# Other TensorE work between a product and its copy-out, and a fixed ScalarE order, in a four-stage kernel

## The chip, the cores and the metric

The kernel runs on one core of a Trainium2 chip. The metric is the time of one execution on the device, in microseconds. Five engines work beside each other, each in the order of its own queue: TensorE (PE, with its weight loads shown as PEld), VectorE (DVE), ScalarE (ACT), GpSimd (POOL) and SyncE (SP), which here issues the transfers. TensorE writes to PSUM; ScalarE and VectorE read it from there.

## The reference, cut to what matters

Four images of 512 channels and 64 x 64 points go through four layers. All is computed in float32. The change is in the first stage (layer 0) and at the start and end of the last one (layers 2 and 3):

```python
# layer 0: attention over the 4096 points of an image, d = 64
t = einsum('oc,bchw->bohw', w_qkv, x)            # key, query, value: 64 channels each
scores = einsum('bdk,bdq->bkq', key_, query)
attn = softmax(scores, axis=1)
out = einsum('bdk,bkq->bdq', value, attn)
x = scale * einsum('oc,bchw->bohw', w_out, out) + x
# layer 1: a bottleneck block whose weights are mixed from 8 experts by a router on mean(x)
# layer 2: linear attention with softplus features, divided by its norm
# layer 3: x + gamma * gate * sigmoid(discounted cumulative sums along rows and columns)
```

## The kernel before, where the change touches it

An image is held as four pairs of 512-point blocks, `xs[0]` to `xs[3]`. Keys and queries of two pairs at a time are computed as a 2 x 2 block product with seven multiplications in place of eight. `self.w[k]` are sums of weights, `term(.., k, ..)` sums of x. Four of the seven (1, 6, 7, 4) are added up in one PSUM bank `y`, and between them `y` is copied out as it stands: `seed` after 1, `e2` after 6, `e3` after 7. The next product goes on adding in the same bank, so it waits until the copy has read it. The three others (5, 2, 3) are added up in `zy`.

```python
class Projections:
    ...
        def steps(self, b):
            first = "v1 cp01 v2 5 1 seed t6 t4 n5 6 e2 2 c11 n6 tr01 7 e3 c22 v3a n7 4 c21 3 c12 n4"
            if b == 0:
                first = "zero v0 1 seed t5 v1 cp01 t6 5 2 c11 t7 t4 n5 6 e2 n6 tr01 v2 7 e3 c22 v3a n7 4 c21 3 c12 n4"
            return first.split(), "5 1 seed 6 e2 2 c11 v3b cp23 7 e3 c22 tr23 4 c21 3 c12".split()
    ...
    def products(self, xs, pair, steps, key, qry, vt):
        ...

            def to_key(src, pr, own=True):
                for h in range(2):
                    n0 = (2 * pr + h) * NB
                    for to in range(2):
                        if own or to != h:
                            nc.scalar.copy(key[to * D:(to + 1) * D, n0:n0 + NB], src(h, n0))
        for step in steps:
            ...
                if step == "zero":

                    nc.tensor.matmul(zy[:, 0, :], ident, wqkv_sb.rearrange("p k o -> p (k o)")[:, 0:NB],
                                     start=True, stop=True)
                elif step.isdigit():
                    k = int(step)
                    to = y if k in (1, 6, 7, 4) else zy[:, 0 if k == 2 else 1, :]
                    for c in range(2):
                        for h in range(2):
                            nc.tensor.matmul(to[h * D:(h + 1) * D, :], self.w[k][:, c, :],
                                             self.term(xs, pair, k, c)[:, h * NB:(h + 1) * NB],
                                             start=c == 0 and k in (1, 5), stop=c == 1,
                                             skip_group_check=k not in (1, 5))
                elif step == "seed":
                    nc.scalar.copy(zy[:, 0, :], y)
                elif step in ("e2", "e3"):
                    e[step] = block(f"{step}_{self.b}_{pair[0]}")
                    nc.scalar.copy(e[step], y)
                elif step == "c11":
                    to_key(lambda h, n0: zy[h * D:(h + 1) * D, 0, :], pair[0])
                elif step == "c12":
                    for h in range(2):
                        r, n0 = slice(h * D, (h + 1) * D), (2 * pair[1] + h) * NB
                        nc.vector.tensor_tensor(key[r, n0:n0 + NB], zy[r, 1, :], e["e2"][r, :], ALU.add)
                    to_key(lambda h, n0: key[h * D:(h + 1) * D, n0:n0 + NB], pair[1], own=False)
                elif step == "c21":
                    nc.vector.tensor_copy(qry[:, pair[0] * NB:(pair[0] + 1) * NB], y)
            ...
```

The steps are words: a digit is one product (four matmuls of 64 x 512), `v` a value product of a pair (eight matmuls), `cp` and `tr` the copy and the transposes of values, `t` and `n` the sums of x on VectorE for this pair and for the next one, `c11` to `c22` the copies of finished blocks to `key` and `qry`. VectorE and ScalarE run this part in program order, TensorE the whole kernel.

Then come the scores, in groups of six, and with each group the value matmuls of the group before:

```python
        def pool(pr, kc):
            xm = xs[pr][:, kc, :]
            nc.scalar.activation(xm, xm, AF.Copy, accum_out=pool_acc[:, kc, pr:pr + 1])
        ...
        for g, group in enumerate(groups):
            for i in group:
                scores(i)
            if 1 < g < 2 + 2 * KC:
                pool(NPAIR - 2 + (g - 2) // KC, (g - 2) % KC)
            if g == 0:
                if b == 0:
                    router_of_values()
                continue
            for _ in range(2):
                if late and late[0][0] < g:
                    late.pop(0)[1]()
            for n, i in enumerate(groups[g - 1]):
                if g == len(groups) - 1 and n == 4:
                    inverse_sums(NPAIR - 1)
                pr = values(i)
                if pr is not None:
                    late.append((g, lambda pr=pr: sums(pr)))
                    if pr < NPAIR - 2:
                        late += [(g + 1, lambda pr=pr, m=m: out_step(pr, m)) for m in range(KC)]
```

`scores(i)` makes two matmuls into one of three PSUM pair buffers, an exp on ScalarE into a ring of twelve, and an addition on VectorE. ScalarE's order here is chosen by the scheduler. `router_of_values` transposes `w_out`, has VectorE copy it, and multiplies it by the router's weights.

The last layer runs through tiles. Its products are seven again, for the sums (`s`) and for the gates (`g`) of a tile, and their orders are lists of words, in which `q` takes a leftover of layer 2 and `v` the first value product of the next image:

```python
        steps = (("s1", "s seed", "l rows 1"), ("g1", "g seed", "y", "l rows 0", "l turn 1"),
                 ("s5", "l turn 0", "a", "q"), ("g5", "l columns 1"),
                 ("s6", "s copy_out 2", "l columns 0", "y"), ("g6", "g copy_out 2", "l sigmoid 1", "a"),
                 ...
        last_steps = (("g5", "l rows 1", "l rows 0"), ("g1", "g seed"), ("g6", "g copy_out 2", "l turn 1"), ("g2",),
                      ("g7", "g copy_out 3", "l columns 1", "g fourth", "l turn 0", "l columns 0", "l sigmoid 1",
                       "l sigmoid 0", "v"), ("g4",), ("g3", "x", "g third", "g first", "g second"))
```

Here `y` is a product of layer 2 into a pair buffer and `a` its addition to x on VectorE (L827). In the second round of tiles the last `q` is the division by the norm: a matmul `nrm` (L760) into a pair buffer and a multiply on VectorE (L763).

## Time and profile before

| | |
|---|---|
| time, median of 3 runs | 2700.67 us (2700.61 to 2700.9) |
| span of the profiled execution | 2698.4 us |
| mean TensorE clock granted | 0.997 |
| matmul `s` of the scores, L354, busy | 466.9 us |
| first score matmul, batch 0 and batch 1 | 56.63 us and 730.50 us |
| transfers, mean over the span | 43 GB/s |

The profile gives each engine's busy time and its share of the span. Its timeline lists instructions in order of time: start, duration, engine, line of the kernel, operation, written tile <- read tiles, shapes, and a count where alike ones are merged. In brackets stands how long the engine was idle before, and what released it. A float32 matmul appears as two records, so a count of 8 is four matmuls of the program. Starts tell more than durations, since matmuls overlap. The granted clock is the share of full speed that TensorE was allowed.

### The profile page before, as it was taken

How to read it: one execution, taken by the hardware profiler on the slowest of the kernel's cores; microseconds unless marked ns; L12 is line 12 of the kernel's file. 1: busy time of each engine (PE TensorE's matmuls, PEld its weight loads, DVE VectorE, ACT ScalarE, POOL GpSimd, SP SyncE). 2: the span in 40 equal slices, each digit the busy share in tenths (PEclk: the TensorE clock that was granted, in tenths of full speed). 3: DMA queues.
4: the chain of work that ended last, by engine and by line, in shares of the span. 5: the costliest groups of instructions: out<-in, count | busy, mean ns of one | idle time of the engine just before them, and what ended most of it. 6: DMA issues, size and time to landing. Idle time of an engine off the chain costs nothing.

```text
span 2698.4 us, 25783 instructions
## 1 busy us (share of the span) xinstructions
PE 2650.6 (98%) x10048; PEld 1114.0 (41%) x10048; DVE 2013.2 (75%) x2270; ACT 1318.2 (49%) x1511; POOL 11.8 (0%) x26
## 2 busy tenths in 40 slices
PE   7999999999999999999999999999999999999998
PEld 2333365344333346434433334543443333554443
DVE  5678766788678876678877878668886777856787
ACT  4555353545655435345565453535556555353545
POOL 1000000000000000000000000000000000000000
PEclk9999999999999999999999999999999999999999
DMA  5000210022200021002220002001121000210011
GB/s 190 1 1 1 102 32 1 16 90 82 94 1 1 1 102 32 1 24 101 78 78 1 0 1 102 32 1 59 66 84 72 0 1 1 102 32 0 32 47 48
DMA packets 34595, 115.17 MB, mean 43 GB/s; under 512 B 2976, under 2 KB 12192, under 8 KB 32928
## 3 DMA queue, kind: packets, MB, share of 16 engines
q1 hardware_dynamic: 34464, 113.43, 11.2%
q8 instruction: 81, 1.33, 0.2%
q14 instruction: 50, 0.41, 0.0%
HBM read 79.86 MB, written 33.55 MB: 42 GB/s over the span
## 4 chain that ended last, share of the span: by engine, by line
PE 89%; DVE 5%; ACT 4%; DMA 1%; issue 1%; SPq 0%; DVEq 0%; ACTq 0%
PE av L369 17%; PE s L354 17%; PE sx L904 14%; PE zy L904 10%; PE z L648 4%; PE c L623 4%; PE c L551 4%; PE c L600 3%; PE wv L822 2%; PE y L413 2%; PE g L724 2%; PE xtr L709 2%; PE kq L296 2%; PE c2e L600 2%; PE vv L252 1%; DVE s L937 1%
## 5 line engine op out<-in xcount | busy, mean ns | idle before, releaser
L354 PE MATMUL s<-qv,key 64*128 64x512 f32 x2048 | 466.9, 602 | 3.4 <-ACT ring L357 3.4
L362 DVE TENSOR_TENSOR acc<-acc,ring 128x1024 f32<-128x1024 f32 x312 | 381.7, 1223 | 95.0 <-ACT ring L357 65.2
L357 ACT ACTIVATE ring<-s 128x1024 f32<-128x1024 f32 x336 | 317.1, 1039 | 210.6 <-PE s L354 210.6
L369 PE MATMUL av<-ring,qv 128*64 128x512 f32 x1344 | 304.5, 595 | 0.0
L354 PEld LDWEIGHTS s<-qv,key 64*128 64x128 f32 x2048 | 188.6, 187 | 279.5 <-issue 171.0
L362 DVE TENSOR_TENSOR acc<-acc,x 128x1024 f32<-128x1024 f32 x168 | 205.6, 1224 | 102.5 <-ACT x L357 89.5
L357 ACT ACTIVATE x<-s 128x1024 f32<-128x1024 f32 x176 | 171.7, 1040 | 203.2 <-PE s L354 203.2
L904 PE MATMUL sx<-t,x 128*128 128x512 f32 x512 | 237.7, 598 | 3.3 <-ACT zy L909 2.5
L369 PEld LDWEIGHTS av<-ring,qv 128*64 128x64 f32 x1344 | 93.3, 137 | 198.6 <-issue 198.6
L369 PE MATMUL av<-x,qv 128*64 128x512 f32 x704 | 167.2, 598 | 0.0
L909 ACT COPY zy<-sx 128x512 f32<-128x512 f32 x64 | 36.5, 570 | 265.8 <-PE sx L904 256.3
L904 PEld LDWEIGHTS sx<-t,x 128*128 128x128 f32 x512 | 95.1, 190 | 133.3 <-issue 117.4
L954 DVE TENSOR_TENSOR_SCAN t<-x,t 128x512 f32<-128x512 f32 x128 | 148.8, 1209 | 1.6
L943 ACT COPY t<-s 128x1024 f32<-128x1024 f32 x64 | 127.5, 1992 | 42.0 <-DVE s L937 41.4
L937 DVE TENSOR_TENSOR_SCAN s<-wc,s 128x512 f32<-128x512 f32 x128 | 146.0, 1202 | 0.0
L913 ACT ACTIVATE e<-sx,prm_sb 128x512 f32<-128x512 f32 x128 | 86.9, 685 | 108.6 <-PE sx L904 108.6
L960 ACT ACTIVATE s<-t 128x1024 f32<-128x1024 f32 x64 | 125.6, 1988 | 12.0 <-DVE t L954 12.0
L904 PE MATMUL zy<-t,wq 128*128 128x512 f32 x256 | 119.3, 604 | 0.0
L904 PE MATMUL sx<-t,wq 128*128 128x512 f32 x256 | 117.0, 597 | 2.1 <-ACT e L913 2.1
L904 PE MATMUL sx<-x,wq 128*128 128x512 f32 x256 | 117.1, 596 | 0.0
L904 PE MATMUL zy<-x,x 128*128 128x512 f32 x256 | 116.2, 594 | 0.0
L648 PE MATMUL z<-x,wqk_sb 128*64 128x512 f32 x512 | 115.9, 597 | 0.0
(229 smaller groups left out, 3443.6 us busy)
## 6 DMA issues: line engine op xcount, KB each, us to landing
out_dram<-s SPq DMA_DIRECT2D x64, 512.0 KB, 2.6
x<-in_x_dram SPq DMA_DIRECT2D x14, 2048.0 KB, 8.6
ex<-in_packed_dram SPq DMA_DIRECT2D x4, 2048.0 KB, 7.5
ex<-in_experts_dram SPq DMA_DIRECT2D x4, 2048.0 KB, 7.8
wq<-in_wproj_t_dram SPq DMA_DIRECT2D x32, 256.0 KB, 5.0
ex<-in_packed_dram SPq DMA_DIRECT2D x4, 1536.0 KB, 6.1
ex<-in_experts_dram SPq DMA_DIRECT2D x4, 1536.0 KB, 6.6
x<-in_packed_dram SPq DMA_DIRECT2D x4, 1536.0 KB, 8.3
```

The source lines that it names most:

```text
L354: nc.tensor.matmul(s[:, h, :], key[r, kt * P:(kt + 1) * P], qry[r, pr * NB:(pr + 1) * NB], start=True, stop=True)
L357: nc.scalar.activation(p, s, AF.Exp)
L362: nc.vector.tensor_tensor(accs[pr], accs[pr], p, ALU.add)
L369: nc.tensor.matmul(avs[pr][h * D:(h + 1) * D, :], vt[:, kt, :], ring[i % RING][:, h, :], start=kt == 0, stop=kt == NT - 1)
L551: nc.tensor.matmul(y[:, h, :], wc[:, kc, :], xs[pr][:, kc, h * NB:(h + 1) * NB], start=kc == 0, stop=kc == KC - 1)
L600: nc.tensor.matmul(y[:, lo - a:hi - a], u, v[:, lo:hi], start=dy == 1, stop=dy == 2)
L648: nc.tensor.matmul(z[h * D:(h + 1) * D, i, :], wqk_sb[:, kc, w * D:(w + 1) * D], xs[pair[i]][:, kc, h * NB:(h + 1) * NB], start=kc == 0, s ...
L904: nc.tensor.matmul(y, w[:, c, self.kind, self.j * P:(self.j + 1) * P], v[:, c, :], start=c == 0 and k in (1, 5), stop=c == 1, skip_group_c ...
L937: nc.vector.tensor_tensor_scan(self.half(i, h), along[:, self.j + 2 * i, :], self.half(i, h), 0.0, ALU.mult, ALU.add)
L943: nc.scalar.copy(self.t[i].rearrange("p (w r) -> p w r", w=W), self.s[i].rearrange("p (r w) -> p w r", w=W))
L954: nc.vector.tensor_tensor_scan(th, down[:, i, :], th, 0.0, ALU.mult, ALU.add)
L960: nc.scalar.activation(self.s[i].rearrange("p (r w) -> p w r", w=W), tw, AF.Sigmoid)
```

## The change

It gives each product that follows a copy of its own partial sum some other TensorE work to do first. In the first stage's step lists, `v2` comes between 1 and 6 and the transposes between 7 and 4. In the second pair of pairs half a value product comes behind 1. The key copies through SBUF (`c12`) are put off, to the place of `k` and behind the first group of exps. VectorE takes `c22` ahead of sums for later products. In the last layer half of the value product moves behind `g1`, and `q` moves one product later.

ScalarE is held to program order in the score loop too, so the pooling passes and key copies stand where the program has them. For the first batch, whose data come while it starts, the order is its own: parameters are loaded ahead of x, the zeroing matmul reads only the identity, and the router's product follows the first values.

```diff
-    xs = [load_pair(0, pr) for pr in range(NPAIR)]
-
-    a11, a12, a21, a22 = (...)
-    nc.vector.tensor_tensor(a21, a21, a22, ALU.add)
     prm_sb = const.tile([P, NPRM], F32, tag="prm", name="prm_sb")
     nc.sync.dma_start(prm_sb, prm)
+    xs = [load_pair(0, pr) for pr in range(NPAIR)]
+
+    a11, a12, a21, a22 = (...)
     ...                                     # after the constants:
+    nc.vector.tensor_tensor(a21, a21, a22, ALU.add)
     ...                                     # router_of_values: the product is returned, with a buffer of its own
+        def products():
+            wr = pair_psum("wr_p")[:, 0, 0:E]
     ...                                     # Projections.steps
-            first = "v1 cp01 v2 5 1 seed t6 t4 n5 6 e2 2 c11 n6 tr01 7 e3 c22 v3a n7 4 c21 3 c12 n4"
+            first = "v1 cp01 5 1 seed v2 t6 t4 n5 6 n6 e2 2 7 e3 c11 c22 tr01 n7 4 c21 3 c12 n4"
             if b == 0:
-                first = "zero v0 1 seed t5 v1 cp01 t6 5 2 c11 t7 t4 n5 6 e2 n6 tr01 v2 7 e3 c22 v3a n7 4 c21 3 c12 n4"
-            return first.split(), "5 1 seed 6 e2 2 c11 v3b cp23 7 e3 c22 tr23 4 c21 3 c12".split()
+                first = "zero v0 1 seed t5 v1 cp01 t6 5 2 t7 t4 6 e2 v2 7 e3 c11 c22 tr01 n5 n6 n7 4 c21 3 c12 n4"
+            return first.split(), "5 1 seed k v3a 6 e2 2 v3b cp23 7 e3 c11 c22 tr23 4 c21 3 c12".split()
     ...                                     # products: zero
-                    nc.tensor.matmul(zy[:, 0, :], ident, wqkv_sb.rearrange("p k o -> p (k o)")[:, 0:NB],
-                                     start=True, stop=True)
+                    nc.tensor.matmul(zy[:, 0, :].rearrange("p (j c) -> p j c", c=P), ident,
+                                     ident[:, None, :].to_broadcast([P, TPB, P]), start=True, stop=True)
     ...                                     # products: c12, and the new step k
-                    to_key(lambda h, n0: key[h * D:(h + 1) * D, n0:n0 + NB], pair[1], own=False)
+                    self.left.append(lambda: to_key(lambda h, n0: key[h * D:(h + 1) * D, n0:n0 + NB], pair[1],
+                                                    own=False))
+                elif step == "k":
+                    self.key_copies()
     ...                                     # the score loop
+        with tc.manual_schedule(engines={mybir.EngineType.Activation}):
             for g, group in enumerate(groups):
                 ...
                 if g == 0:
+                    pro.key_copies()
                     if b == 0:
-                        router_of_values()
+                        router = router_of_values()
                     continue
                 ...
+                if b == 0 and g == 1:
+                    router()
     ...                                     # the last layer
-                 ("s5", "l turn 0", "a", "q"), ("g5", "l columns 1"),
+                 ("s5", "l turn 0", "a"), ("g5", "l columns 1", "q"),
     ...
-        last_steps = (("g5", "l rows 1", "l rows 0"), ("g1", "g seed"), ...
+        last_steps = (("g5", "l rows 1", "l rows 0"), ("g1", "g seed", "v 0"), ...
-                       "l sigmoid 0", "v"), ...
+                       "l sigmoid 0", "v 2"), ...
-                            pro.value(nxt, 0)
+                            pro.value(nxt, 0, int(args[0]), 2)
```

More of the change, by code (lines that the diff above doesn't have):

```diff
@@ L99, in unshifted @@
     nc.sync.dma_start(wqkv_sb, wqkv_t.rearrange("(kc p) o -> p kc o", p=P))
-    xs = [load_pair(0, pr) for pr in range(NPAIR)]
-    a11, a12, a21, a22 = (wqkv_sb[:, k:k + 2, w * D:(w + 1) * D] for w in range(2) for k in (0, 2))
-    nc.vector.tensor_tensor(a21, a21, a22, ALU.add)
     prm_sb = const.tile([P, NPRM], F32, tag="prm", name="prm_sb")
@@ L107, in col @@
         return prm_sb[:, i:i + n]
+    xs = [load_pair(0, pr) for pr in range(NPAIR)]
+    a11, a12, a21, a22 = (wqkv_sb[:, k:k + 2, w * D:(w + 1) * D] for w in range(2) for k in (0, 2))
     wout_sb = const.tile([P, C], F32, tag="wout", name="wout_sb")
@@ L173, in router_of_values @@
         nc.vector.tensor_copy(wot_sb, wo_t[:, 0, :])
-        for kc in range(KC):
-            nc.tensor.matmul(wo_t[:, 1, 0:E], wot_sb[:, kc * P:(kc + 1) * P], router_sb[:, kc, :],
-                             start=kc == 0, stop=kc == KC - 1)
-        nc.vector.tensor_scalar(wr_sb, wo_t[:, 1, 0:E], col(SCALE), 1.0 / HW, ALU.mult, ALU.mult)
+        def products():
+            wr = pair_psum("wr_p")[:, 0, 0:E]
+            for kc in range(KC):
+                nc.tensor.matmul(wr, wot_sb[:, kc * P:(kc + 1) * P], router_sb[:, kc, :],
+                                 start=kc == 0, stop=kc == KC - 1)
+            nc.vector.tensor_scalar(wr_sb, wr, col(SCALE), 1.0 / HW, ALU.mult, ALU.mult)
+        return products
     def load_experts(b, j, n, pool, tag, pack=True):
@@ L214, in __init__ @@
             self.sums = bigp.tile([P, 4, 2, NB], F32, tag="big", name=f"ring_{b}")
-            self.fours, self.vv, self.vsb = [], {}, {}
+            self.fours, self.vv, self.vsb, self.left = [], {}, {}, []
         def sum_weights(self):
@@ L225, in steps, with key_copies @@
         def steps(self, b):
[L226 removed]
+            first = "v1 cp01 5 1 seed v2 t6 t4 n5 6 n6 e2 2 7 e3 c11 c22 tr01 n7 4 c21 3 c12 n4"
             if b == 0:
[L228 to L229 removed]
+                first = "zero v0 1 seed t5 v1 cp01 t6 5 2 t7 t4 6 e2 v2 7 e3 c11 c22 tr01 n5 n6 n7 4 c21 3 c12 n4"
+            return first.split(), "5 1 seed k v3a 6 e2 2 v3b cp23 7 e3 c11 c22 tr23 4 c21 3 c12".split()
+        def key_copies(self):
+            while self.left:
+                self.left.pop(0)()
         def term(self, xs, pair, k, c):
@@ L434, in layer0 @@
         late = []
-        for g, group in enumerate(groups):
-            for i in group:
-                scores(i)
-            if 1 < g < 2 + 2 * KC:
-                pool(NPAIR - 2 + (g - 2) // KC, (g - 2) % KC)
-            if g == 0:
-                if b == 0:
-                    router_of_values()
-                continue
-            for _ in range(2):
-                if late and late[0][0] < g:
-                    late.pop(0)[1]()
-            for n, i in enumerate(groups[g - 1]):
-                if g == len(groups) - 1 and n == 4:
-                    inverse_sums(NPAIR - 1)
-                pr = values(i)
-                if pr is not None:
-                    late.append((g, lambda pr=pr: sums(pr)))
-                    if pr < NPAIR - 2:
-                        late += [(g + 1, lambda pr=pr, m=m: out_step(pr, m)) for m in range(KC)]
+        with tc.manual_schedule(engines={mybir.EngineType.Activation}):
+            for g, group in enumerate(groups):
+                for i in group:
+                    scores(i)
+                if 1 < g < 2 + 2 * KC:
+                    pool(NPAIR - 2 + (g - 2) // KC, (g - 2) % KC)
+                if g == 0:
+                    pro.key_copies()
+                    if b == 0:
+                        router = router_of_values()
+                    continue
+                for _ in range(2):
+                    if late and late[0][0] < g:
+                        late.pop(0)[1]()
+                for n, i in enumerate(groups[g - 1]):
+                    if g == len(groups) - 1 and n == 4:
+                        inverse_sums(NPAIR - 1)
+                    pr = values(i)
+                    if pr is not None:
+                        late.append((g, lambda pr=pr: sums(pr)))
+                        if pr < NPAIR - 2:
+                            late += [(g + 1, lambda pr=pr, m=m: out_step(pr, m)) for m in range(KC)]
+                if b == 0 and g == 1:
+                    router()
         assert not [t for t in late if t[0] < len(groups) - 1], late
@@ L999, in layer3 @@
                        ("s3", "s second"))
-        last_steps = (("g5", "l rows 1", "l rows 0"), ("g1", "g seed"), ("g6", "g copy_out 2", "l turn 1"), ("g2",),
+        last_steps = (("g5", "l rows 1", "l rows 0"), ("g1", "g seed", "v 0"), ("g6", "g copy_out 2", "l turn 1"), ("g2",),
                       ("g7", "g copy_out 3", "l columns 1", "g fourth", "l turn 0", "l columns 0", "l sigmoid 1",
-                       "l sigmoid 0", "v"), ("g4",), ("g3", "x", "g third", "g first", "g second"))
+                       "l sigmoid 0", "v 2"), ("g4",), ("g3", "x", "g third", "g first", "g second"))
         pro = None
```

## The prediction, made before the changed kernel ran

> **What bounds the kernel now.** I read the busy totals first, then the chain that ended last, then TensorE's timeline for the whole span, keeping only the rows with an idle time, and last ScalarE's timeline around the largest of those gaps. The totals and the head of the chain:
>
> ```profile
> PE 2650.6 (98%) x10048; PEld 1114.0 (41%) x10048; DVE 2013.2 (75%) x2270; ACT 1318.2 (49%) x1511; POOL 11.8 (0%) x26
> PE 89%; DVE 5%; ACT 4%; DMA 1%; issue 1%; SPq 0%; DVEq 0%; ACTq 0%
> ```
>
> TensorE is busy for all but 2698.4 - 2650.6 = 47.8 us. The change adds no arithmetic and takes almost none away, so those 47.8 us, and matmuls run at a reduced clock, are all it can win: 54 us, the 2%, is out of reach. TensorE's timeline shows where some of the idle time is. Batch 0, then batch 1 (batches 2 and 3 repeat it to 0.02 us):
>
> ```profile
> 30.59 1.94 PE L296 MATMUL kq<-ring,wqkv_sb 128*64 128x512 f32 x8 [0.59 <-ACT e L304]
> 34.35 1.94 PE L296 MATMUL kqz<-x,kqw 128*64 128x512 f32 x8 [1.82 <-DVE qv L315]
> 42.57 3.51 PE L296 MATMUL kq<-ring,kqw 128*64 128x512 f32 x8 [2.85 <-ACT kqz L301]
> 53.05 1.94 PE L296 MATMUL kq<-ring,wqkv_sb 128*64 128x512 f32 x8 [0.80 <-ACT e L304]
> 56.63 2.85 PE L354 MATMUL s<-qv,key 64*128 64x512 f32 x12
> 60.33 2.94 PE L354 MATMUL s<-qv,key 64*128 64x512 f32 x12 [0.85 <-ACT ring L357]
> 67.21 1.87 PE L175 MATMUL wo_t<-router_sb,wot_sb 128*128 128x8 f32 x8 [3.35 <-DVE wot_sb L173]
> ...
> 497.53 1.13 PE L760 MATMUL nrm<-inv,spread 32*128 32x512 f32 x4 [1.18 <-DVE x L827]
> ...
> 678.08 1.98 PE L904 MATMUL sx<-t,x 128*128 128x512 f32 x4 [0.66 <-ACT zy L909]
> 702.00 1.94 PE L296 MATMUL kq<-ring,kqw 128*64 128x512 f32 x8 [0.67 <-ACT kqz L301]
> 718.01 1.94 PE L296 MATMUL kq<-ring,kqw 128*64 128x512 f32 x8 [0.87 <-ACT kqz L301]
> 726.92 1.94 PE L296 MATMUL kq<-ring,wqkv_sb 128*64 128x512 f32 x8 [0.79 <-ACT e L304]
> 734.20 8.40 PE L354 MATMUL s<-qv,key 64*128 64x512 f32 x36 [0.85 <-ACT ring L357]
> ```
>
> Start, duration, line, in brackets the idle time and its releaser. Each gap at L296 is a product that waits until its own partial sum has been copied out (`seed` L301, `e2`/`e3` L304). The 2.85 us at 42.57 are more than one copy: ScalarE, in order, first did this:
>
> ```profile
> 39.56 1.30 ACT L282 COPY key<-key 64x512 f32<-64x512 f32 x2
> 40.88 1.06 ACT L431 ACTIVATE x<-x 128x1024 f32<-128x1024 f32 x1
> 41.85 0.19 ACT L431 ACTIVATION_READ_ACCUMULATOR x<-x 128x1 f32 x1
> 41.94 0.58 ACT L301 COPY kqz<-kq 128x512 f32<-128x512 f32 x1
> ```
>
> The product ended at about 39.7; key copies and a pooling pass (L431) stood ahead of the seed.
>
> **What the Trainium skill says.** "TensorE: Matmul & The Clock Gate", What's actually happening: the array runs at half clock after an idle window of some 3.4 us and at full clock after as long a busy one. The trace agrees in kind: after 2.85 us idle eight matmuls took 3.51 us against 1.89, and after the 3.35 us at 67.21 the next 24 scores took 7.35 (chain) against 5.35. "ScalarE: Activation LUTs", What ACT_TABLE_LOAD costs: about 1283 ns a load; here 1.28 (23.33 and 28.66, around the square root of L153, ahead of an `e3`). "SBUF — State Buffer", two separate sides: a GpSimd instruction and a VectorE one with two SBUF inputs lock each other out. Agrees: the two subtractions at 34.21, beside GpSimd's L120 (31.61 to 37.81), took 4.08 together; the same kind took 2.35.
>
> **The change part by part.** Units from the timeline: a product of eight 1.72 us, a value product 3.43 (half: 1.72), a value transpose 1.05, a 512-wide copy 0.58, two SBUF subtractions 2.35, a score 0.89, an exp 0.92 to 0.93 in a run (3.73 for four).
>
> *Batches 1 to 3, from the last tile of the stage before.* Half a value product now stands behind `g1`; it covers its seed (0.57), so the 0.66 goes. But `g6`, its `copy_out`, `turn` and the scans behind start 1.0 later (half a product 1.72 minus the 0.66). Hence the last sigmoid ends at 694.7 instead of 693.8, the table load at 696.0, the two value copies at about 697.1. The second value product, now between `1` and `6`, takes over the PSUM buffer that these copies free (its instruction in the built program waits for ScalarE). TensorE reaches it at 696.85: a new wait of about 0.25. It covers the seed (0.67 gone). I put `6` at 700.6 (702.00 before: 1.4 won). Then `2` 702.4, `7` 704.15, transposes 705.9, `4` 706.95: `e3` is done at 706.7. `3` at 708.7 needs `c22` on VectorE, behind four subtractions that wait for the load of pair 3. That load is issued when the last scan ends (691.57, now 692.5) and lands 10.6 later plus issue, 703.4; 703.4 + 4.6 + 0.65 = 708.7, just in time. The pair (2,3): 7 x 1.72 + 3.43 + 1.05 with some 0.09 per wait or switch puts the first score at 727.5 (730.50 before: 3.0). Every copy there has at least 1.05 us of other work behind it, and the key copies that held the first exp (731.97 to 733.2) now stand behind six exps. They then delay exp 7 by 1.2, of which TensorE sees about 1.0 in the first twelve scores (before 0.85 plus 0.3 stretch). Won per batch: 3.1, all three 9.3.
>
> *Batch 0.* From 16.64, the end of the second value product's issue, I add 0.4 for the parameter load now ahead of x (25 KB, issue slot 0.5) and for the clock, since the zeroing product now needs only the identity (ready at 1.4) and will be over before x lands. So 17.05. Then 5, 2, 6: 22.2; v2 25.7; 7 27.4; transposes 28.4; 4 30.2; 3 31.9; 5, 1, v3a 37.0; 6 38.8; 2, v3b 42.2. The subtractions for pair 3 are now behind `c22` and the value copies, so they start at 30.05, not 26.97, and run into GpSimd's L120: I take them to be held some 3.4 us (the lock from 32.4 to 35.8). 6 just manages, but `c12` ends at about 42.3, the key copies at 43.5, and `e2` stands behind them, 44.1: `7` waits 1 to 1.8. Then 7, transposes, 4, 3 = 6.2, and the first score at about 50.5 against 56.63: 6.1 won. Gone are 0.59 + 1.82 + 2.85 + 0.80 and the 1.79 lost to the clock (7.85); up to 1.8 come back.
>
> From first score to first values product 19.8 us passed before (56.63 to 76.44). Now: twelve scores and four transposes are 11.3; the third of the ring's PSUM buffers waits for VectorE's copy of `wo_t` (at about 8.3 + 0.7 after the first score, behind four additions of 1.33), 1.2; exp pace the rest, in all 12.6. The router products come after the values, some 0.6. 19.8 - 13.2 = 6.6 won, 2.0 of it the clock.
>
> *Stage four.* The nrm matmul waits 1.18 for the buffer that L827 reads; one product (1.72) later it is free. Its own reader on VectorE now follows two scans: value_add ends 497.4, scans 499.7, the multiply 500.85, and the next `y`, which takes the buffer, is due at 500.8: even. 1.1 per batch, 4.4.
>
> Moved off the path: the eight pooling passes (1.25 each) now follow the exps of groups 2 to 9; a group costs TensorE 10.65 and ScalarE 6 x 0.93 + 1.25 = 6.8.
>
> Sum: 6.1 + 6.6 + 9.3 + 4.4 = 26.4; 2700.7 - 26.4 = 2674.3, rounded to 2674.5.
>
> **Rivals.** (1) The copies were not what held batches 1 to 3 but the load of pair 3 (VectorE idles for it at 702.50, 2.83 us). For it: `3` is due the moment `c22` ends, and the load is issued later than before. Against: TensorE reaches nothing that needs it before 708. If it binds, 1 us per batch less: 2678. (2) ScalarE's fixed order in the score loop turns against it: a copy of av waits for TensorE and the exps behind it wait too. For: 12 av copies waited 27.2 us in all, longest 4.0. Against: ScalarE has 3.8 us spare in each group and av ends in the first part of the values. If wrong by 0.5 us in each of 22 x 4 groups: 2718. (3) Batch 0 stays bound by the transfers (213 GB/s over 60 us, pair 3 only at 26.85) and by GpSimd's lock, and the early zeroing leaves the array cold at x: 4 to 5 us of the 12.7 stay: 2679. (4) Everything hides better than I think, batch 0's first score at 48.5 and the 0.25 and 1.0 absent: 2669.
>
> **Range and chances.** Batches 1 to 3 and stage four rest on gaps that repeat to 0.02 us, so their 13.7 is uncertain by about 3; batch 0 by 4; a lapse such as rival 2 is unlikely. 2667.5 to 2683 should hold it 8 times in 10. More than 2% faster needs 2646.7, more than the idle time allows with the starting wait kept; 0.01. Slower by 2% would take a new wait in every group: 0.01. Within 2%: 0.98.
>
> **What would show it.** The gaps before L296 (now L304) by ACT gone or under 0.3 us in batches 1 to 3; first score of batch 0 near 50.5, its first values 13 us later with no half-clock stretch between; nrm's 1.18 gone and no wait at the next wv; TensorE's busy time down by 3 to 5 us (clock) and idle by about 22. I am wrong if new waits of over 1 us stand at `3`, at the second value product or at the wv products, if scores wait for exps in the middle of the loop, or if the first batch's products run at half clock again.

## The result and the profile after

| | before | after |
|---|---|---|
| median of the runs beside each other (6 and 6) | 2700.35 us (2699.67 to 2700.90) | 2683.80 us (2682.47 to 2685.98) |
| ratio | | 0.9939, 95% interval 0.9926 to 0.9952 |
| span of the profiled execution | 2698.4 us | 2684.2 us |
| TensorE busy / idle in it | 2650.6 / 47.8 us | 2648.0 / 36.2 us |
| first score of batch 0 at | 56.63 us | 57.30 us |
| from the first score of batch 1 to that of batch 2 | 666.15 us | 663.61 us |

The kernel is 0.6% faster: "within 2%", as predicted, but 9.3 us above the predicted 2674.5 and 0.8 us outside the range. (The profiled execution of the changed kernel was the slowest of its six.) The page's totals and the head of its chain of waits, after the change:

```profile
PE 2648.0 (99%) x10048; PEld 1112.5 (41%) x10048; DVE 2013.3 (75%) x2270; ACT 1314.3 (49%) x1510; POOL 12.1 (0%) x26
PE 90%; DVE 5%; ACT 4%; issue 1%; DMA 0%; SPq 0%; DVEq 0%; ACTq 0%
```

The arithmetic is the same; 2.6 us of busy time and 11.6 us of idle time are gone, where the prediction had 3 to 5 and about 22. TensorE's timeline after the change, again rows with an idle time, batch 0 and then batch 1 (L304 is a product, L326 `c22`, L252 a subtraction of x tiles, L365 a score):

```profile
6.78 6.01 PE L260 MATMUL vv<-x,wqkv_sb 128*64 128x512 f32 x16 [3.24 <-DMA x<-in_x_dram]
...
32.03 1.94 PE L304 MATMUL kqz<-x,kqw 128*64 128x512 f32 x8 [0.77 <-DVE qv L326]
37.77 3.02 PE L304 MATMUL kqz<-ring,wqkv_sb 128*64 128x512 f32 x8 [3.80 <-DVE ring L252]
40.57 2.62 PE L304 MATMUL kq<-x,wqkv_sb 128*64 128x512 f32 x8
...
55.44 1.94 PE L304 MATMUL kqz<-x,kqw 128*64 128x512 f32 x8 [0.77 <-DVE qv L326]
66.44 3.71 PE L365 MATMUL s<-qv,key 64*128 64x512 f32 x16 [1.18 <-DVE wot_sb L173]
...
690.83 3.65 PE L260 MATMUL vv<-x,wqkv_sb 128*64 128x512 f32 x16 [0.23 <-ACT vsb L266]
703.30 1.94 PE L304 MATMUL kqz<-x,kqw 128*64 128x512 f32 x8 [0.77 <-DVE qv L326]
720.91 1.94 PE L304 MATMUL kqz<-x,kqw 128*64 128x512 f32 x8 [0.77 <-DVE qv L326]
731.82 2.94 PE L365 MATMUL s<-qv,key 64*128 64x512 f32 x12 [1.04 <-ACT x L368]
```

What the change was made for has happened: no gap before a product in the first stage is by `seed`, `e2` or `e3` any more, and the 1.18 us before nrm and the 0.66 us before `g6` are gone. But there is a wait that the prediction does not have: product 3, twice in every batch, 0.77 us, by `c22`. In batch 0 a larger one follows, 3.80 us by the subtractions for pair 3, and two products at a reduced clock behind it (3.02 and 2.62 us; 5.25 us from start to start of the next work instead of 3.44).

The timeline of the other engines around the first of these waits says what `c22` itself waited for (L290 is a key copy, four of which make `c11`; L277 copies transposed values; L119 is a GpSimd multiplication by gamma):

```profile
28.41 0.58 ACT L312 COPY e<-kq 128x512 f32<-128x512 f32 x1 [4.57 <-PE kq L304]
28.90 2.35 ACT L290 COPY key<-kqz 64x512 f32<-64x512 f32 x4
31.28 0.69 DVE L326 TENSOR_TENSOR qv<-kqz,e 128x512 f32<-128x512 f32 x1 [8.48 <-ACT key L290]
31.89 1.28 DVE L277 COPY qv<-vtr 128x512 f32<-128x512 f32 x2
33.09 5.67 DVE L252 TENSOR_TENSOR ring<-x,x 128x1024 f32<-128x1024 f32 x2
32.83 5.44 POOL L119 TENSOR_SCALAR wv_sb<-wv_sb,prm_sb 128x2048 f32<-128x2048 f32 x1 [31.36 <-DMA bv_sb<-in_bv_dram]
```

`e3` is done at 28.9, yet `c22` starts at 31.28, when the four key copies of `c11` are over. `c11` reads one half of the PSUM pair tile `kqz`, `c22` the other, and the profile names a key copy (L290) as what released `c22`. So the subtractions start at 33.09, 0.26 us behind GpSimd's L119, and two of them take 5.67 us instead of 2.35.

**The theory:** the readers of one PSUM pair tile are served one after another, and product 3, which writes the second half again, waits for the last of them; with `c11` named ahead of `c22` this costs 2 x 0.77 us a batch, and in batch 0 the meeting with GpSimd besides. **The rivals:** in batches 1 to 3 the load of pair 3 holds `c22` in any case; in batch 0 GpSimd's multiplications are the cause, whenever `c22` comes; and the early zeroing leaves TensorE cold at the start. (The letters of a quoted expectation are explained in it.) Two parts were also tried alone, and one part undone.

### The profile page after: what moved, and what is told of

Read it like the earlier page. It is cut to its first block, busy times and chain, and to the rows that moved or that the text cites. A ratio compares the mean times of both kernels' runs of the same rounds, so it can differ in the third digit from the quotient of the medians.

```text
span 2684.2 us, 25782 instructions
## 1 busy us (share of the span) xinstructions
PE 2648.0 (99%) x10048; PEld 1112.5 (41%) x10048; DVE 2013.3 (75%) x2270; ACT 1314.3 (49%) x1510; POOL 12.1 (0%) x26
## 4 chain that ended last, share of the span: by engine, by line
PE 90%; DVE 5%; ACT 4%; issue 1%; DMA 0%; SPq 0%; DVEq 0%; ACTq 0%
PE av L380 17%; PE s L365 16%; PE sx L919 14%; PE zy L919 10%; PE z L663 4%; PE c L638 4%; PE c L566 4%; PE c L615 3%; PE wv L837 2%; PE y L424 2%; PE g L739 2%; PE xtr L724 2%; PE vv L260 2%; PE c2e L615 2%; PE kqz L304 1%; PE kq L304 1%
## 5 line engine op out<-in xcount | busy, mean ns | idle before, releaser
L365 PE MATMUL s<-qv,key 64*128 64x512 f32 x2048 | 463.9, 598 | 4.3 <-ACT x L368 3.1
L365 PEld LDWEIGHTS s<-qv,key 64*128 64x128 f32 x2048 | 189.1, 186 | 276.2 <-issue 173.6
```

The lines of the kernel that those rows point to most:

```text
L365: nc.tensor.matmul(s[:, h, :], key[r, kt * P:(kt + 1) * P], qry[r, pr * NB:(pr + 1) * NB], start=True, stop=True)
```

## The experiments

For each run: the first score of batch 0, the two intervals from first score to first score (batches 1 to 2 and 2 to 3), all from the profile, and the median and ratio to the kernel before. Each ratio is to executions of the kernel before made beside the run; their medians are 2699.20 to 2700.35 us, so medians of different rows compare to about 1 us. Of the kernels made from the changed one, only two have an interval clear of the changed kernel's: the one with late key copies, and all together. For the others the argument rests on the traces; beside it, the executions with `c11` moved (2677.30 to 2679.18 us) all lie below those of the changed kernel (2682.47 to 2685.98).

| kernel | first score | intervals | median | ratio (95%) |
|---|---|---|---|---|
| before | 56.63 | 666.15, 666.19 | 2700.35 | 1 |
| after | 57.30 | 663.61, 663.61 | 2683.80 | 0.9939 (0.9926 to 0.9952) |
| `c22` named first | 53.01 | 665.62, 667.69 | 2685.54 | 0.9949 (0.9932 to 0.9965) |
| no gamma on GpSimd | 51.89 | 663.63, 663.64 | 2680.63 | 0.9932 (0.9916 to 0.9949) |
| both | 51.52 | 664.93, 664.83 | 2685.65 | 0.9951 (0.9935 to 0.9968) |
| old zeroing | 56.66 | 663.65, 663.65 | 2685.49 | one run |
| `c11` moved | 52.38 | 663.63, 663.33 | 2677.63 | 0.9918 (0.9902 to 0.9935) |
| and gamma on ScalarE | 49.38 | 662.47, 664.50 | 2677.55 | 0.9918 (0.9902 to 0.9935) |
| and late key copies, router, zeroing x5 | 48.95 | 661.82, 661.31 | 2670.17 | 0.9890 (0.9874 to 0.9907) |
| product 2 ahead of 6 | 57.69 | 661.79, 662.56 | 2679.84 | 0.9929 (0.9913 to 0.9944) |
| all together | 49.24 | 660.36, 660.43 | 2667.17 | 0.9882 (0.9867 to 0.9897) |
| after, loop order free | 54.89 | 664.15, 664.14 | 2688.04 | 0.9960 (0.9945 to 0.9976) |
| before, q moved | 55.58 | 664.91, 664.95 | 2694.42 | 0.9981 (0.9974 to 0.9988) |
| before, v split | 54.11 | 665.89, 665.92 | 2698.44 | 0.9998 (0.9990 to 1.0007) |

**`c22` named ahead of `c11`.** All three step lists of the changed kernel:

```diff
-... 7 e3 c11 c22 tr01 ...
+... 7 e3 c22 c11 tr01 ...
```

> The changed kernel with c22 named ahead of c11 in all step lists, so that VectorE's addition waits for e3 alone and the four key copies follow it. Theory (c22 was made to wait for the four key copies, 2.35 us of ScalarE): both gaps of 0.77 us at product 3 (L304) vanish in every batch, 1.5 us each in batches 1 to 3, and in batch 0 the subtractions for pair 3 start at about 30.8 instead of 33.1, the 3.80 us gap ahead of product 5 shrinks below 1 us and the first score comes 3 to 4 us earlier, at about 53.5. In all some 8 us: about 2676 us. Rival A (the load of pair 3 and the subtractions ahead of c22 hold it): gaps unchanged in batches 1 to 3, 2683 us. Rival B (only GpSimd's lock matters in batch 0): 4.6 us gained, batch 0's gap stays at 3.8, about 2679 us.

2685.54 us, not distinguishable from the changed kernel. In batch 0 it did what was expected (first score 53.01), but the wait of product 3 had only changed its name. Timeline of this run, batch 1:

```profile
696.96 0.68 DVE L326 TENSOR_TENSOR qv<-kqz,e 128x512 f32<-128x512 f32 x1
697.67 2.36 ACT L290 COPY key<-kqz 64x512 f32<-64x512 f32 x4 [1.70 <-DVE qv L326]
700.08 1.94 PE L304 MATMUL kqz<-x,kqw 128*64 128x512 f32 x8 [1.85 <-ACT key L290]
```

Now the key copies wait for `c22`, and the product for the key copies. `c22` stands on VectorE behind four subtractions that need the load of pair 3, so what was 0.77 us in the first passes of batches 1 to 3 became 1.85, 2.54 and 2.92 us (in the second passes 0.90). My theory of this run, "`c22` must come first", was wrong: it is the pair of readers, in either order, that must be over, and the load of pair 3 does hold the product as soon as both readers hang on it.

**The multiplications by gamma left out.** The changed kernel without them; this leaves out a multiplication of wv and its bias:

```diff
-    nc.gpsimd.tensor_scalar(wv_sb, wv_sb, col(GAM2), None, ALU.mult)
-    nc.gpsimd.tensor_scalar(bv_sb, bv_sb, col(GAM2), None, ALU.mult)
```

> The changed kernel without GpSimd's two multiplications of wv and bv by gamma (L119, L120; left out: the factor gamma, which is 1 here). Theory (GpSimd's read of wv stretches VectorE's two-input subtractions): the two subtractions for pair 3 take 2.4 instead of 5.67 us, start unchanged at about 33.1, product 5 starts at about 34.4 instead of 37.8 and at full clock (1.72 per product instead of 2.8 and 2.45), first score at about 52 instead of 57.3; the 0.77 gaps stay. About 2678.5 us. Rival (the subtractions wait for the transfer of x, and GpSimd is beside the point): unchanged, 2683 us.

2680.63 us, 3.2 us under the changed kernel by the medians (the intervals of the ratios overlap). Its timeline in batch 0:

```profile
31.52 1.94 PE L302 MATMUL kqz<-x,kqw 128*64 128x512 f32 x8 [0.76 <-DVE qv L324]
33.94 2.12 PE L302 MATMUL kqz<-ring,wqkv_sb 128*64 128x512 f32 x8 [0.48 <-DVE ring L250]
32.58 2.35 DVE L250 TENSOR_TENSOR ring<-x,x 128x1024 f32<-128x1024 f32 x2
```

The subtractions take 2.35 us, the gap of 3.80 shrinks to 0.48, the clock stays, and the first score comes 5.4 us earlier; the 0.76 us by `c22` stays. Batches 1 to 3 do not change (663.63), so this is about batch 0 alone.

**Both of these.**

> Both edits: c22 ahead of c11, and no multiplications on GpSimd (the factor gamma, 1 here, is left out). If the two causes are independent outside batch 0 and share batch 0's wait: no gap above 0.3 us at L304 in batches 1 to 3, first score of batch 0 at about 49.5 to 50.5 (as I had predicted for the changed kernel), about 2672 to 2674 us. If a third cause holds batch 0: first score above 52, 2676 us or more.

2685.65 us: first score 51.52, only 0.4 us earlier than without the multiplications alone, and batches 1 to 3 1.2 us longer, for the reason just given. The two edits remove the same wait in batch 0 (4.3 and 5.4 us alone, 5.8 together); their effects do not add.

**The old zeroing matmul.** The changed kernel with the zeroing product reading wqkv again, so that it runs later:

```diff
-  nc.tensor.matmul(zy[:, 0, :].rearrange(...), ident, ident[:, None, :].to_broadcast([P, TPB, P]), ...)
+  nc.tensor.matmul(zy[:, 0, :], ident, wqkv_sb.rearrange("p k o -> p (k o)")[:, 0:NB], ...)
```

> The changed kernel with the zeroing matmul reading wqkv again, so that it runs at about 4.4 to 6.4 us and the array has no idle time before x. Theory (the early zeroing left the array at half clock when x came: first value product 6.01 us long, product 1 at 12.62 against 11.49 before): the value product takes about 5 us and product 1 starts at about 11.9. Rival (the parameter transfer ahead of x is the delay): product 1 stays at 12.6. The total moves by less than 1 us either way, since batch 0 is held later.

One run, 2685.49 us. TensorE's timeline:

```profile
4.45 2.05 PE L297 MATMUL kqz<-wqkv_sb,ident 128*128 128x512 f32 x2 [4.45 <-DVE wqkv_sb L126]
7.17 5.39 PE L260 MATMUL vv<-x,wqkv_sb 128*64 128x512 f32 x16 [0.67 <-DMA x<-in_x_dram]
```

The idle time before x fell from 3.24 to 0.67 us, but product 1 started at 12.39 instead of 12.62: 0.2 us, not the 0.7 that I gave to the cold array. The cold start is worth little, as far as one execution can say: over the profiles of all kernels with the new order of loads product 1 starts at 11.93 to 14.00 us.

**The key copies elsewhere.** The changed kernel, `c11` moved and nothing else: behind `e2` (batch 0, first pass), to the end (batches 1 to 3, first pass), behind product 2 (second pass):

```diff
-"v1 cp01 5 1 seed v2 t6 t4 n5 6 n6 e2 2 7 e3 c11 c22 tr01 n7 4 c21 3 c12 n4"
+"v1 cp01 5 1 seed v2 t6 t4 n5 6 n6 e2 2 7 e3 c22 tr01 n7 4 c21 3 c12 n4 c11"
-"... t7 t4 6 e2 v2 7 e3 c11 c22 tr01 ..."
+"... t7 t4 6 e2 c11 v2 7 e3 c22 tr01 ..."
-"5 1 seed k v3a 6 e2 2 v3b cp23 7 e3 c11 c22 tr23 4 c21 3 c12"
+"5 1 seed k v3a 6 e2 2 c11 v3b cp23 7 e3 c22 tr23 4 c21 3 c12"
```

> Only the four key copies of product 2's half (c11) move in ScalarE's order: right after e2 in the first pass of batch 0, to the end of the first pass in batches 1 to 3, right after product 2 in every second pass. No other operation changes place. Theory (product 3 waits for every reader of the PSUM pair tile that it shares with product 2, and the key copies were the late reader): neither pass of any batch has more than 0.2 us before product 3 (0.77 after the change, 0.9 to 2.9 with c22 named first); the first score of batch 0 comes at about 51.5 us (57.30), batches 1 to 3 take about 662.0 us each (663.6), in all 6.0 + 3 x 1.55 = 10.6 less: 2673. Rival A (c22 is held by the subtractions that wait for the load of pair 3, whatever ScalarE does): a gap of 0.8 us or more stays before the first product 3 of batches 1 to 3, about 2675.5. Rival B (GpSimd's multiplications hold the first batch whenever the subtractions of pair 3 come): product 6 or 5 of batch 0 still waits 2 us or more, first score at 53.5 or later, 2675 or more.

2677.63 us, 6.2 us under the changed kernel, where 10.6 were expected. Its timeline, TensorE in batch 0 and batch 2, then VectorE's `c22` in batch 0, ScalarE in batch 1 and VectorE's subtractions in batch 0:

```profile
44.85 1.94 PE L304 MATMUL kq<-ring,kqw 128*64 128x512 f32 x8 [1.22 <-ACT e L312]
47.72 1.15 PE L273 MATMUL vtr<-ident,vsb 128*128 128x128 f32 x8 [0.93 <-ACT vsb L266]
...
1368.17 1.94 PE L304 MATMUL kq<-ring,kqw 128*64 128x512 f32 x8 [1.31 <-ACT kqz L309]
...
29.18 0.69 DVE L326 TENSOR_TENSOR qv<-kqz,e 128x512 f32<-128x512 f32 x1 [7.51 <-ACT e L312]
...
701.53 2.36 ACT L290 COPY key<-kqz 64x512 f32<-64x512 f32 x4 [6.17 <-DVE key L318]
...
33.28 5.79 DVE L252 TENSOR_TENSOR ring<-x,ring 128x1024 f32<-128x1024 f32 x2
```

The 0.77 us before product 3 are gone in both passes of all batches (one of 0.16 us is left, in batch 2), `c22` now follows `e3` at once (29.18, released by L312), and the first score of batch 0 is 4.9 us earlier. That is the theory. What I missed looks like the same rule once more: at the end of the pass `c11` waits for another reader of its tile, `c12` on VectorE (6.17 us by L318; both also write `key`, so this run does not say which of the two shared tiles makes it wait), and then holds the second seed, 1.31 us before product 6 in batches 2 and 3. In batch 0 the multiplication by gamma still holds a pair of subtractions (5.79 us), `c12` comes late, and `e2` with it: 1.22 and 0.93 us.

**Gamma on ScalarE as well.** The multiplications are done, by ScalarE, behind `e3` of the first pass of batch 0:

```diff
-    nc.gpsimd.tensor_scalar(wv_sb, wv_sb, col(GAM2), None, ALU.mult)
-    nc.gpsimd.tensor_scalar(bv_sb, bv_sb, col(GAM2), None, ALU.mult)
+                elif step == "gam":
+                    nc.scalar.activation(wv_sb, wv_sb, AF.Copy, scale=col(GAM2))
+                    nc.scalar.activation(bv_sb, bv_sb, AF.Copy, scale=col(GAM2))
```

> As the kernel with the key copies moved, and the two multiplications by gamma (128x2048 and 128x512) go from GpSimd to ScalarE, behind e3 of the first pass of batch 0, where ScalarE is idle for over 10 us. Theory: with the subtractions of pair 3 starting near 30.8 instead of 33.09, the lock with GpSimd is mostly off the path, so this brings at most 0.5 us over the moved key copies alone; the subtractions take 2.35 us a pair; first score at 51.0, total 2672.5. Rival B (GpSimd's lock is what remains of batch 0): first score 2 us or more earlier than with the key copies alone, total 2 us or more below it. Rival C: ScalarE's multiplications (estimate 3 us from 32 on) come in the way of the second seed, which would show as a gap before product 6 by ScalarE.

The GpSimd rival was right about batch 0: the first score comes at 49.38, 3.0 us before that of the run above. Timeline:

```profile
32.94 2.35 DVE L250 TENSOR_TENSOR ring<-x,ring 128x1024 f32<-128x1024 f32 x2
32.23 2.00 ACT L307 ACTIVATE wv_sb<-wv_sb,prm_sb 128x2048 f32<-128x2048 f32 x1 [3.38 <-DMA wv_sb<-in_wv_t_dram]
...
2021.70 1.94 PE L302 MATMUL kqz<-x,kqw 128*64 128x512 f32 x8 [1.03 <-DVE qv L327]
```

ScalarE does in 2.00 us, beside full-speed subtractions, what took GpSimd 5.44 to 7.47 us in the runs above and below, and no gap stands in batch 0 between x and the scores. But the median, 2677.55, is that of the run above: in its profile product 6 waits 1.31 us in batch 1 too (0.53 in batch 2, 1.31 in batch 3), and batch 3 has 1.03 us before product 3, by `c22`, which the load of pair 3 held. The load takes over there when everything else comes earlier.

**The part "q" alone, on the kernel before.**

```diff
-("s5", "l turn 0", "a", "q"), ("g5", "l columns 1"),
+("s5", "l turn 0", "a"), ("g5", "l columns 1", "q"),
```

> The kernel before with one part of the change alone: in stage four the steps q go from s5 to behind g5. Theory: the 1.18 us before the nrm matmuls go in each of four batches and nothing takes their place, 4.4 to 4.7 us less than before: 2695.8. Rival: the next y or wv product waits instead for the same PSUM buffer, gaps of 1 us there, and the time stays within 1 us of 2700.3.

2694.42 us, ratio 0.9981 (0.9974 to 0.9988): 5.5 us under the kernel before beside it (2699.95). The intervals shorten by 1.24 us each; four times that is 5.0. TensorE's timeline where 1.18 us stood before:

```profile
496.92 1.13 PE L760 MATMUL nrm<-inv,spread 32*128 32x512 f32 x4
497.98 1.98 PE L904 MATMUL sx<-t,x 128*128 128x512 f32 x4
499.89 1.13 PE L822 MATMUL wv<-wc,kv 64*128 64x512 f32 x4
```

No wait at nrm, and none at the next wv: nothing takes its place.

**The part "v" alone, on the kernel before.**

```diff
-last_steps = (..., ("g1", "g seed"), ..., "l sigmoid 0", "v"), ...
+last_steps = (..., ("g1", "g seed", "v 0"), ..., "l sigmoid 0", "v 2"), ...
```

> The kernel before with one part of the change alone: half of the next batch's first value product goes behind g1 in the last tile. Theory (what the prediction counted): the 0.66 us before g6 go in three batches, the scans and the copies of the value product come 0.9 later, which in this order of steps TensorE does not see: 2.0 less than before, 2698.4. Rival: TensorE sees the later copies in full, a new wait of 0.3 to 1 us at the next value product or the first partial sum in each batch: 2700 or more.

2698.44 us, ratio 0.9998 (0.9990 to 1.0007): no difference that the runs resolve. That the median is the expected 2698.4 is luck: the kernel before beside it had 2699.20, so 0.8 us were won and not 2.0. The profile has 0.26 us per interval:

```profile
695.01 1.94 PE L296 MATMUL kqz<-ring,wqkv_sb 128*64 128x512 f32 x8 [0.23 <-ACT vsb L258]
699.39 1.94 PE L296 MATMUL kq<-ring,kqw 128*64 128x512 f32 x8 [0.72 <-ACT kqz L301]
```

The 0.66 us before `g6` went, and 0.23 us came back at the later value copies, with 0.05 us more at the seed. The new wait is the one that the rival named, though below its 0.3 to 1 us; the rival was nearer.

**The loop's order free again.** The changed kernel, the loop of scores outside the fixed order:

```diff
-        with tc.manual_schedule(engines={mybir.EngineType.Activation}):
+        if True:
```

> The changed kernel with one part undone: ScalarE's order in the loop of scores is left to the scheduler again, as in the kernel before; it then puts the eight pooling passes of 1.25 us back between the copies of the first stage, two of them ahead of the first exp. Theory (the fixed order is what keeps the copies on time, and it costs nothing in the loop): waits by ScalarE of 1 to 3 us come back before products and first values, 2 to 3 us per batch, 2692 to 2695. Rival 2 of the prediction (the fixed order holds exps behind copies of av in the loop): the loop of 22 groups gets shorter by more than the first stage gets longer, 2683 or less.

2688.04 us, 4.2 us over the changed kernel by the medians; the intervals of the ratios overlap. From first score to first score it is 0.54 us longer in batches 1 and 2. Timeline of this run, ScalarE and TensorE in batch 1, then VectorE and GpSimd in batch 0 (L442 is a pooling pass):

```profile
721.42 1.06 ACT L442 ACTIVATE x<-x 128x1024 f32<-128x1024 f32 x1 [1.91 <-PE kqz L304]
...
720.30 1.94 PE L304 MATMUL kqz<-x,kqw 128*64 128x512 f32 x8 [0.93 <-DVE qv L326]
726.00 8.46 PE L365 MATMUL s<-qv,key 64*128 64x512 f32 x36 [0.98 <-ACT ring L368]
...
32.26 2.35 DVE L252 TENSOR_TENSOR ring<-x,x 128x1024 f32<-128x1024 f32 x2
34.53 5.79 DVE L252 TENSOR_TENSOR ring<-x,ring 128x1024 f32<-128x1024 f32 x2
32.37 7.47 POOL L119 TENSOR_SCALAR wv_sb<-wv_sb,prm_sb 128x2048 f32<-128x2048 f32 x1 [30.89 <-DMA wv_sb<-in_wv_t_dram]
```

The pooling passes stand among the copies again, two of them ahead of the first exp, but they mostly fill idle time of ScalarE; the waits they bring are small (0.93 instead of 0.77 us before the second product 3; 0.98 before the first scores, where 1.04 stood a little later). Batch 0 loses more: 14.34 us from its first score to its first values (12.78 in the changed kernel). From the first score of batch 0 to the end the profile is 3.2 us longer. Both expectations were too large: by this profile the fixed order is worth 3.2 us in all, about half a microsecond in each of the later batches. Rival 2 of the prediction, which had the loop suffer from it, falls: from the first score of batch 1 to the output product behind its loop of scores (L424 at 961.30 and 961.61) it is 239.14 us with the free order and 238.83 with the fixed one.

**Further waits removed.** The run with gamma on ScalarE, with the left-over key copies of the second pass behind the exps of the third group, the router one group later, and the zeroing product issued five times:

```diff
-                if g == 0:
+                if g == 2:
                     pro.key_copies()
-                    if b == 0:
-                        router = router_of_values()
+                if g == 0:
                     continue
 ...
                 if b == 0 and g == 1:
+                    router = router_of_values()
+                if b == 0 and g == 2:
                     router()
 ...
+                    for _ in range(5):     # around the zeroing matmul
```

> As the kernel with moved key copies and gamma on ScalarE, and three more: the two key copies left over from the second pass go behind the exps of the third group of scores instead of the first; the transposes of wo and their products one group later; the zeroing matmul is issued five times in a row, so that TensorE has something to do until x lands. Theory: the 1.04 us before scores 7 to 12 go in each batch and the 1.18 us by wot_sb in batch 0; product 1 of batch 0 starts at about 11.5 instead of 12.6, because the first value product then runs at full clock; 4 x 1.0 + 1.2 + 1.0 = 6.2 us less than the kernel with moved key copies and gamma alone, about 2666.5. Rival (the first value product is paced by the chunks of x, and the scores by the exps of 0.93 us against 0.89): product 1 stays at 12.4 or later, half of the score gap comes back, 3 us less at most, 2669.5.

2670.17 us, 7.4 us less than without these three. TensorE's timeline at its start and at the first scores:

```profile
8.37 3.97 PE L258 MATMUL vv<-x,wqkv_sb 128*64 128x512 f32 x16
12.16 1.89 PE L303 MATMUL kq<-x,wqkv_sb 128*64 128x512 f32 x8
...
48.95 10.71 PE L367 MATMUL s<-qv,key 64*128 64x512 f32 x48
```

The twelve scores run through without a gap (10.71 us), so the 1.04 and 1.18 us are gone. Five zeroing products make the value product itself fast (3.97 us instead of 5.74 in the run above), yet product 1 starts only 0.4 us earlier. Some of the 7.4 us is in none of the three terms that were counted: the waits before products 6 and 3 in batches 1 to 3 add up to 4.2 us in the profile of the run above and to 2.4 here.

**Product 2 ahead of product 6.** The changed kernel; in the first pass of batches 1 to 3 and in every second pass the key copies get their place by an exchange of products, in batch 0's first pass behind `e2`:

```diff
-"v1 cp01 5 1 seed v2 t6 t4 n5 6 n6 e2 2 7 e3 c11 c22 tr01 ..."
+"v1 cp01 5 1 seed v2a t6 t4 n5 2 c11 6 n6 e2 v2b 7 e3 c22 tr01 ..."
-"... t7 t4 6 e2 v2 7 e3 c11 c22 tr01 ..."
+"... t7 t4 6 e2 c11 v2 7 e3 c22 tr01 ..."
-"5 1 seed k v3a 6 e2 2 v3b cp23 7 e3 c11 c22 tr23 ..."
+"5 1 seed k v3a 2 c11 6 e2 v3b cp23 7 e3 c22 tr23 ..."
```

> The changed kernel with the products of the first stage in one other order, 2 before 6, so that the four key copies of 2's half run before e2, and half a value product between 6 and 7 for e2 to hide behind (first pass of batches 1 to 3 and every second pass; in batch 0's first pass the key copies move behind e2). GpSimd, loop and stage four as in the changed kernel. Theory (the readers of the PSUM pair tile are served one after another, and product 3 waits for the last): no gap over 0.1 us by c22 before product 3 unless the load of pair 3 holds c22; no second seed later than in the changed kernel (the 1.31 us of the run that put the key copies last). Batch 0's first score at 52.4 as with the key copies moved, batches 1 to 3 each 1.5 less than the changed kernel's 663.6: 2683.8 - 4.9 - 4.6 = 2674.3. Rival (the load of pair 3 takes the place of the wait): gaps of 0.5 to 1 us before product 3 in batches 1 to 3, 2676.5.

2679.84 us: 5.5 above what was expected, and nearly all of it in batch 0, where 1.1 us stand ahead of product 1 already (14.00 instead of 12.90 with `c11` moved; x landed later). Timeline of this run, TensorE and then ScalarE:

```profile
48.32 3.68 PE L304 MATMUL kq<-ring,kqw 128*64 128x512 f32 x8 [3.78 <-ACT e L312]
...
2027.05 1.94 PE L304 MATMUL kqz<-x,kqw 128*64 128x512 f32 x8 [0.66 <-DVE qv L326]
...
44.06 1.34 ACT L290 COPY key<-key 64x512 f32<-64x512 f32 x2 [5.72 <-DVE key L318]
45.31 2.35 ACT L290 COPY key<-kqz 64x512 f32<-64x512 f32 x4
47.68 0.59 ACT L312 COPY e<-kq 128x512 f32<-128x512 f32 x1
```

In batches 1 to 3 it is the theory as written down: no gap at product 3 or at the seed but one of 0.66 us in batch 3 (the load of pair 3), intervals of 661.79 and 662.56 us. In batch 0's second pass `c11` and `e2` stand behind the left-over copies, these behind `c12`, and `c12` behind the subtractions that GpSimd holds: 3.78 us, then a product at half clock.

**All of it together:** that order with gamma on ScalarE, the later groups and the five zeroing products.

> The same order of products with gamma on ScalarE, the left-over key copies and the router product in later groups, and five zeroing matmuls. Theory: the 0.66, 1.17 and 0.60 us that product 6 waited for the second seed in batches 1 to 3 of the best kernel so far go: 2670.2 - 2.4 = 2667.8. Rival (the load of pair 3 then holds c22): half of it comes back before product 3, 2669.0.

2667.17 us, ratio 0.9882 (0.9867 to 0.9897): faster than both kernels, 16.6 us under the changed one. TensorE's timeline in batch 0 and batch 1:

```profile
10.11 1.08 PE L258 MATMUL vv<-x,wqkv_sb 128*64 128x512 f32 x4 [0.16 <-DMA x<-in_x_dram]
11.39 1.08 PE L258 MATMUL vv<-x,wqkv_sb 128*64 128x512 f32 x4 [0.21 <-DMA x<-in_x_dram]
12.30 1.89 PE L303 MATMUL kq<-x,wqkv_sb 128*64 128x512 f32 x8
...
693.42 1.94 PE L303 MATMUL kqz<-x,kqw 128*64 128x512 f32 x8 [0.32 <-DVE qv L328]
```

With the array warm, the first value product waits for the chunks of x themselves, the last at 11.39 us; in the kernel before, the same row, also after a wait for x, stands at 10.58:

```profile
10.58 1.08 PE L252 MATMUL vv<-x,wqkv_sb 128*64 128x512 f32 x4 [0.20 <-DMA x<-in_x_dram]
```

The 0.32 us are what is left before product 3 in batch 1; batches 2 and 3 have no wait there.

## Why the prediction was wrong, and where it was right

**The step that failed.** The prediction let `c22` follow as soon as `e3` is copied: "The subtractions for pair 3 are now behind `c22` and the value copies, so they start at 30.05", "`3` at 708.7 needs `c22` on VectorE [...] just in time", and "Every copy there has at least 1.05 us of other work behind it". The last is true of `e3` and not of `c11`, which the new order moves from behind product 2 to between `e3` and `c22`: 2.35 us of key copies that read the same PSUM tile. They, and not `e3`, end last before product 3. Moving them, and nothing else, took the waits away.

How much it cost can be added up. From 2698.4 - 26.4 = 2672.0 the profiled execution misses 12.2 us: 6.8 in the first stage of batch 0 (57.30 instead of 50.5), 0.6 from there to the router's products (13.8 instead of 13.2), and 1.66 in each of three batches (2.54 won per interval, of a predicted 3.1 + 1.1). In batches 1 to 3 the failed step is 2 x 0.77 = 1.54 of the 1.66; with the exchange of products they fell to 661.79 and 662.56, where the prediction has 666.15 - 4.2 = 661.95. In batch 0 it is the 4.9 us that moving the key copies gave. Together 4.6 + 4.9 = 9.5 of the 12.2 us, worked out from the traces of different runs. Not all of the 4.9 is certain to be `c11`'s: with it GpSimd came first by 0.26 us, but in the run with the loop's order free, which has the late `c22` too, VectorE came first by 0.11. Counted from product 1, the first score came after 44.68 us in the changed kernel, 42.96 in that run and 39.48 with `c11` moved, so some 1.7 of 5.2 us may turn with this meeting from one execution to the next. As a change of the whole kernel it was not had for nothing: two places for `c11` brought 6.2 and 4.0 us, because each gave some back elsewhere.

**Terms that were mis-sized.** The start: "I add 0.4 for the parameter load now ahead of x [...] and for the clock". It was about 1.25 in this profile, since the second value product ended near 17.9 instead of 17.05; in others with the same order of loads it ended between 17.07 and 19.15, so the term is not firm. With TensorE kept busy product 1 started 0.3 to 0.5 us earlier, less than that spread. The last chunk of x was waited for until 11.39 us instead of 10.58; that the parameter load does this was not tried by itself. Batch 0's second pass: "`7` waits 1 to 1.8"; once `c22` was on time the waits there were 1.22 + 0.93 = 2.15 us. The way there was right: subtractions held by GpSimd, then `c12`, the key copies, `e2`. The hold of "some 3.4 us" was 5.67 - 2.35 + 2.76 - 2.35 = 3.7. These two (0.85, and 2.15 instead of the middle 1.4) and the 0.6 are 2.2 of the remaining 2.7 us; 0.5 I cannot place. One small reading was wrong from the start: the 1.79 us lost to the clock is 3.51, a duration, less 1.72, a distance between starts; from start to start it is 45.91 - 42.57 - 1.72 = 1.62. And the first values stood at 76.36 before, not 76.44.

**What held.** The "new wait of about 0.25" at the second value product is 0.23. "About 1.0 in the first twelve scores" is 1.04. From first score to first values 12.6 was predicted and 12.78 measured (70.08 - 57.30), with no half-clock stretch in it. Stage four: 1.1 per batch predicted, 1.24 measured alone. Of the signs of being wrong one came, batch 0's products at a reduced clock; the new wait at `3`, 0.77 us, stayed below the 1 us that the prediction had named as a sign.

**The rivals.** (1) The load of pair 3 does not bind in the changed kernel, where `c22` waits for ScalarE (0.97 to 1.83 us) after the subtractions are done; it binds as soon as that wait is gone and all else is early (0.66 and 1.03 us in batch 3 of two runs). (2) fell. (3) was the nearest, 2679 for a batch 0 held by transfers and GpSimd, but in part by luck. GpSimd does hold batch 0: without its multiplications the first score came 5.4 us earlier. But it was the late `c22` that made the meeting cost 5.6 us; with `c22` on time it cost 2.15. Neither it nor the sum had the wait in batches 1 to 3. The chances of the three classes were right, and were nearly fixed by the idle time alone.

## What to carry to other kernels

Before a copy is given a slot by its own data, list every reader of the whole buffer that the next product writes, on all engines, and put the last of them in the path: in this program, with a tile of two PSUM banks, a copy of the other bank was part of that list. A wait that goes to the neighbour when two steps are exchanged (`c22` by `c11`, then `c11` by `c22`) says that the set of readers is the limit, so one of them has to leave the stretch. And where two edits remove the same wait, measure them alone and together before adding their gains: in batch 0 4.3 and 5.4 us made 5.8.

## What the runs showed of the hardware that was not expected

- Where VectorE's subtractions and GpSimd's multiplication met, a quarter of a microsecond decided who paid. VectorE at 32.26 and GpSimd at 32.37: the pair of subtractions took 2.35 us, and the next pair 5.79. GpSimd at 32.83 and VectorE at 33.09: the first pair took 5.67. Some 3.4 us are lost either way, but only in the second case by the subtractions that TensorE waits for first. "SBUF — State Buffer", two separate sides, of the Trainium skill says that whichever starts first has the shared ports for its whole instruction; the traces agree, though in the first case not one but two subtractions went through ahead of GpSimd. I had put the lock at a fixed place in time (32.4 to 35.8) and not asked who would be first.
- An idle window of the same length did not always bring the half clock. In the kernel before, a product of eight took 3.51 us after 2.85 us idle, and 3.43 after the same wait in the run with only q moved. In the run with only v split it took 1.94 us, and the first score came 2.5 us earlier with nothing changed in batch 0:

```profile
41.62 1.94 PE L296 MATMUL kq<-ring,kqw 128*64 128x512 f32 x8 [2.85 <-ACT kqz L301]
```

A gain of that size in the first stage of batch 0 can therefore not be read from one profile; the 4.9 us of the moved key copies are above it, the differences of 1 us and less between starts are not.
- `c11` and `c22` read different PSUM banks, and in the traces the second still waits for the first (released by L290 in the changed kernel, by L326 with the two exchanged). "PSUM — Partial Sum Buffer", PSUM bank collisions raise a hardware error, asks for such an order between two engines on one bank, and has accesses to different banks run side by side. No run here tests that; with the two halves in tiles of their own the wait might not have been there, which stays open.
